# Moving weight sums and token sums of a Strassen-like MLP between stages of a one-core transformer block

## The chip, the cores and the metric

The kernel runs on one core of one Trainium2 chip. The metric is the device time of one execution in microseconds. The profile is of one further execution, whose own time is given beside the time of the others.

## The reference

A conditioned transformer block on x of shape (2, 2048, 512) in float32: two rows of 2048 tokens, width 512 (D), 16 heads of 32, hidden width 2048.

```python
mod = silu(condition) @ Wada + bada
sh_a, sc_a, gt_a, sh_m, sc_m, gt_m = split(mod, 6)
xm = layernorm(x) * (1 + sc_a) + sh_a
x = x + gt_a * attention(xm)          # causal softmax, 16 heads, then @ Wproj + bproj
xm = layernorm(x) * (1 + sc_m) + sh_m
h = gelu(xm @ W1 + b1)                # exact gelu
x = x + gt_m * (h @ W2 + b2)
```

## The kernel before

**Order of the work.** For each row: QKV (in four groups g of 512 tokens), attention, projection. Behind both rows comes the MLP, four times (m = 0 to 3) over 1024 tokens. The order on each engine is written out by hand: `act` and `mm` keep an instruction in program order, and helpers named `among`, `also`, `between` and `then` hang other work behind a numbered step of the main loop. All DMAs on SP are issued in program order too; GpSimd (POOL) issues the others from its own queue, in which its additions stand as well.

**The MLP.** Both layers are block products with seven instead of eight multiplications (the Winograd form of Strassen's scheme), applied twice: seven outer products, named A11, S1, A12, S2, S3, S4, A22 after the weight operand, each of seven inner products (`seven`), each of those 4 weight tiles times 256 tokens. Operands are sums of blocks:

- Weight sums: a piece of a layer has seven blocks, four loaded and three summed in four steps (`room_sum`, L1222, 128x512 in a full room). The outer sums were made earlier and lie in DRAM as `w1d`, `w2d`; complete pieces lie in `w1e`, `w2e`. Three pieces of W1 are completed in row 1's QKV (`FirstLayer`, at steps 1, 7 and 13 of its 48), four in row 1's attention in halves (`FirstHalves`, through `beside`). All seven of W2 are completed in m=0 of the MLP: `Weights.load` fetches four blocks, `Weights.add` puts the four sums on POOL during the outer product before the one that needs them, and then stores the piece in `w2e` for m = 1 to 3. For these, SP loads each piece in two parts.
- Token sums of the first layer: each outer operand needs four inner sums of 128x256 (`inner_x`, 28 for each m). One is made per inner product, for the coming outer product, on POOL, or on VectorE (DVE) while the outer products S3 and S4 (numbers 4 and 5) run.
- Token sums of the second layer (`Hidden`): sums of 128x1024 on DVE (`pop`). Four of them may be made within the first layer, from outer product 5 on, when no inner sum of the coming product is left.

All these sums are recorded at L1586 (`difference`). In the first layer, DVE adds each product's PSUM banks to a tile (`combine`, L1713), two evictions for each inner product. In the outer products S2 and S3, POOL adds every new block to another one (also L1713, `h<-h,h`), and where an eviction is a copy by ScalarE (ACT), POOL makes the addition (L1941, `c<-c,h`). The inner products write to the bank pairs `ps_a`, `ps_b` and `ps_c`; `ps_a` is added to several times, so the seventh inner product waits for the eviction of the fifth, the fifth for that of the third.

**Attention.** For each unit of 512 queries and four heads there are row scores (`s`, for the maxima, DVE reduces them) and transposed scores (`st`, for the exponentials by ACT). Row scores run ahead, in a list `row.todo`; when it is empty there are none left. Each step of 128 keys opens four `st` banks with a small matmul (`st<-fold,sel`) and waits for their last exponentials. `st_bank` gives them four banks, and in the last unit two more, those of `s`. A few row scores run already in QKV: `among` puts them between its matmuls. In the last value product of the last group it left out the place before the last matmul, so that the scores due there came behind it. Row 1's attention keeps its tiles where the rooms of row 1's QKV lay.

Of the kernel before, what the change touches and what calls it, by code (L numbers as in the profile page):

```python
# [17 lines left out]
P = 128  # L18
# [9 lines left out]
def dit_block_kernel(  # L28
# [540 lines left out]
    def attention_phase(row, beside=None):  # L569
        b, vv, kst, qst = row.b, row.vv, row.kst, row.qst  # L570
        with pool(f"att{b}") as ap, pool(
# [7 lines left out]
            def scores_t(u, step, n, behind_rows):  # L579

                def st_bank():

                    n_bank[0] += u == len(units) - 1
                    if n_bank[0] % 6 >= HC:
                        return ps_sp.tile([P, QB], F32, tag="s", name="st")
                    return ps_stp.tile([P, QB], F32, tag="st", name="st")

                c, i = units[u]
                tiles = steps_of[u][step]
                q0 = tiles[0][1]
                w = sum(QB - q for _, q in tiles)
                sts, es = [], []  # L600
                for h in range(HC):
                    g = slice(h * HD, (h + 1) * HD)
                    st = st_bank()
                    mm(
                        st[:, :w], sel[g, :], fold[u % 2][g, q0 : q0 + w],
                        start=True, stop=False,
                    )
                    sts.append(st)
                narrow = w < QB or u == 0
                if n > HC:  # L610
                    row.score(1)
                for h in range(HC):
                    at = 0
                    for j, q in tiles:
                        mm(
                            sts[h][:, at : at + QB - q],
                            kst[c][:, h, j * P : (j + 1) * P],
                            qst[u][:, h, q:],
                            start=False, stop=at + QB - q == w,
                        )  # L620
                        at += QB - q
                    if h % 2 == 0:
                        e = ap.tile([P, 2, QB], F32, tag="e", name="e", bufs=E_BUFS // 2)
                        es.append(e)
                    act(nc.scalar.activation(e[:, h % 2, :w], sts[h][:, :w], AF.Exp))  # L625
                    if tiles[0][0] >= i * TQ and (h % 2 or len(tiles) > 1):

                        if len(tiles) > 1:
                            d = e[:, h % 2, :].rearrange("p (t k) -> p t k", k=P)
                            d = d[:, 0 : TQ : TQ - 1, :]  # L630
                        else:
                            d = e[:, :, :P]
                        act(
                            nc.gpsimd.affine_select(  # L634
                                d, d, pattern=[[0, 2], [1, P]],
                                compare_op=ALU.is_ge, fill=0.0,
                                base=0, channel_multiplier=-1,
                            )
                        )
# [87 lines left out]
            for u, (c, i) in enumerate(units):  # L727
# [5 lines left out]
                for n_step, tiles in enumerate(steps_of[u]):  # L733
# [77 lines left out]
                        pending.append((now + LAG, lambda u=u, o=o, sm=sm: finish(u, o, sm)))  # L811
                    pending.sort(key=lambda p: p[0])
                    if among:
                        among(now, n_step >= i * TQ, u + 1 == len(units))
                    now += 1
            flush(now + LAG)

# [2 lines left out]
    class Qkv:  # L820
# [241 lines left out]
        def run(self, hp, also):  # L1062
# [3 lines left out]
            for g in range(NG):  # L1066
# [104 lines left out]
                )  # L1171
            )

    def beside(pieces):

        def start(pool_):

            room = pool_.tile([P, piece], F32, tag="w7", name="w7")
            todo = []

            def among(now, slack, last):
                if not todo and pieces.left():
                    todo.append((now + 3 if now else 0, "load"))
                elif not todo:
                    return
                after, what = todo[0]
                if now < after:
                    return
                if what == "load":
                    todo.pop(0)  # L1190
                    pieces.load(room, nc.sync)
                    todo[:] = [(now + 3, n) for n in range(4)]
                elif what == "store":
                    todo.pop(0)
                    pieces.store(nc.sync)
                elif slack or last:
                    todo.pop(0)
                    pieces.make((what,))
                    if what == 3:
                        todo.append((now + 1, "store"))  # L1200
# [27 lines left out]
            room[:, 2:6], src.rearrange("p k (i f) d -> p (k i) (f d)", i=2)  # L1228
        )

    class FirstLayer:

        def __init__(self, rooms):
            self.rooms, self.at, self.made, self.stored = rooms, 0, 0, 0

        def load(self):  # L1240

            act(load_blocks(nc.gpsimd, self.rooms[self.at % 2], 1, self.at))
            self.at += 1

        def make(self):

            room = self.rooms[self.made % 2]
            for k in range(4):
                room_sum(room, 1, k)
            self.made += 1  # L1250

        def store(self):

            act(nc.gpsimd.dma_start(w1e[self.stored], self.rooms[self.stored % 2]))
            self.stored += 1

    class FirstHalves:


        def __init__(self, first):  # L1260
            self.at, self.loaded, self.made = 2 * first, [], []

        def left(self):
            return self.at < 14

        def load(self, room, queue):
            n, half = self.at // 2, self.at % 2
            self.at += 1
            w = room.rearrange("p (n d) -> p n d", n=7)
            src = w1d[:, n].rearrange("p k (i f) d -> p (k i) (f d)", i=2)  # L1270
            act(queue.dma_start(w[:, 2:6], src[:, :, half * 2 * P : (half + 1) * 2 * P]))
            self.loaded.append((n, half, w))

        def make(self, steps):

            for step in steps:
                room_sum(self.loaded[0][2], 1, step)
                if step == 3:
                    self.made.append(self.loaded.pop(0))

        def store(self, queue):

            n, half, w = self.made.pop(0)
            act(queue.dma_start(w1e[n][:, :, half * 2 * P : (half + 1) * 2 * P], w))

    def project_phase(row, psum, between):

# [208 lines left out]
    attention_phase(row, beside(quarters))  # L1496
    assert quarters.at == FC and not quarters.loaded and not quarters.made


# [1 line left out]
    with pool("qkv1") as qp, pool("ps_qkv1", bufs=6, space=PSUM) as ps_mm:  # L1501
# [20 lines left out]
        with pool("hl1") as hp:  # L1522
            room = [
                hp.tile([P, 7, C * P], F32, tag=f"w49{n}", name="w49") for n in range(2)
            ]
            late = FirstLayer(room)

            def also(g, n):
                at = g * (C * 2 + MTT) + n
# [9 lines left out]
            assert late.stored == 3  # L1539

    halves = FirstHalves(late.stored)
    attention_phase(row, beside(halves))
    assert not halves.left() and not halves.loaded and not halves.made
    ps_s_cm.__exit__(None, None, None)

# [4 lines left out]
    with ExitStack() as mlp:  # L1550
# [58 lines left out]
        class Weights:  # L1609
# [6 lines left out]
            def load(self, at, part):  # L1616
# [135 lines left out]
        class Hidden:  # L1752
# [110 lines left out]
            def first_layer(self, among):  # L1863
# [37 lines left out]
                def one_outer(at, n, dst, base):  # L1901
# [61 lines left out]

                    def then(k):
                        self.gelu()
                        if todo and todo[0][0] <= at + 1:
                            inner_x(at)
# [277 lines left out]
```

## Time and profile before

| | |
|---|---|
| Runs | 2245.97, 2245.99, 2253.21 us (median 2245.99) |
| Profiled execution, own time | 2247.44 us |
| Its span, mean granted TensorE clock | 2245.7 us, 0.999 |
| TensorE busy | 2224.7 us (99%) |
| DVE, ACT, POOL busy | 1572.5, 977.6, 1301.1 us |
| QKV, attention of row 1 from | 775, 953 us |
| First layer of m=0 from | 1528.8 us |

A row of the timeline has start and duration in us, engine, line, operation, output and inputs, shape and count, and in brackets the idle time before it with what ended it. A row of a group has, behind the bars, busy us and mean ns, and idle time before it.

### The profile page before, as it was taken

To read this page: it belongs to the slowest core of one execution; us is meant where nothing else is said; L and a number is where in the kernel's file an instruction comes from. 1 tells how busy PE (TensorE), PEld (TensorE's weight loads), DVE (VectorE), ACT (ScalarE), POOL (GpSimd) and SP (SyncE) were. 2 spreads that over 40 slices of the span, in tenths; PEclk is the share of its full clock that TensorE was granted. 3 is DMA by queue.
4 is the path that set the end of the run, shared out by engine and by line. 5 is a ranking of instruction groups with operands and counts; after the bars stand their busy time and mean duration, and the time that the engine had idled before them with its cause. 6 is when DMAs were issued, how large, how long until landed. Compare 5 with 4: busy or idle time off the path is not lost.

```text
span 2245.7 us, 34452 instructions
## 1 busy us (share of the span) xinstructions
PE 2224.7 (99%) x12429; PEld 1442.5 (64%) x12429; DVE 1572.5 (70%) x3172; ACT 977.6 (44%) x1909; POOL 1301.1 (58%) x1052
## 2 busy tenths in 40 slices
PE   8999999999999999999999999999999999999999
PEld 3676555555544457655555555447888888888887
DVE  3467777777776526677777777745996876877787
ACT  3334555555555134255555555723422342252230
POOL 4362997989793550079897998373764602602510
PEclk9999999999999999999999999999999999999999
DMA  8769226262245777551623315465466554654643
GB/s 282 248 208 240 61 64 153 55 149 74 66 158 167 246 243 209 165 126 50 149 74 74 99 50 166 148 231 202 145 254 225 190 188 145 216 181 150 217 147 121
DMA packets 144515, 355.66 MB, mean 158 GB/s; under 512 B 14625, under 2 KB 44877, under 8 KB 130649
## 3 DMA queue, kind: packets, MB, share of 16 engines
q1 hardware_dynamic: 137632, 316.72, 47.3%
q0 software_dynamic: 6336, 36.20, 4.4%
q8 instruction: 98, 1.61, 0.3%
q14 instruction: 73, 0.59, 0.1%
q10 hardware_dynamic: 376, 0.55, 0.1%
HBM read 253.80 MB, written 107.48 MB: 161 GB/s over the span
## 4 chain that ended last, share of the span: by engine, by line
PE 93%; DVE 5%; issue 1%; ACT 0%; DMA 0%; ACTq 0%; DVEq 0%
PE st L204 19%; PE ps_a L204 15%; PE o L204 12%; PE s L204 10%; PE ps_b L204 7%; PE ps_o L204 5%; PE ps_v L204 5%; PE sm L204 4%; PE ps_u L204 4%; PE ps_c L204 4%; PE ps_w L204 3%; PE ps_qk L204 3%; PE ps_xt L212 1%; DVE sum L1586 1%; DVE h L1713 1%
## 5 line engine op out<-in xcount | busy, mean ns | idle before, releaser
L625 ACT ACTIVATE e<-st 128x512 f32<-128x512 f32 (+1 forms) x1152 | 570.0, 579 | 384.1 <-PE st L204 348.5
L481 DVE TENSOR_REDUCE mx<-s 128x1 f32<-128x512 f32 x618 | 420.5, 688 | 179.3 <-PE s L204 176.3
L666 POOL TENSOR_TENSOR ee<-ee,e 128x1024 f32<-128x1024 f32 x204 | 480.0, 2385 | 7.4 <-ACT e L625 7.4
L204 PE MATMUL s<-kst,qst 128*128 128x512 f32 (+3 forms) x1028 | 425.2, 417 | 2.7 <-DVE mx L481 1.5
L204 PE MATMUL st<-qst,kst 128*128 128x512 f32 (+3 forms) x1280 | 377.5, 379 | 0.0
L204 PE MATMUL ps_a<-sum,room 128*128 128x256 f32 x1504 | 356.7, 381 | 3.2 <-DVE c L1713 1.5
L204 PEld LDWEIGHTS ps_a<-sum,room 128*128 128x128 f32 x1504 | 280.8, 190 | 52.3 <-issue 6.0
L204 PE MATMUL o<-e,vv 128*32 128x512 f32 (+3 forms) x2560 | 300.8, 537 | 0.0
L204 PEld LDWEIGHTS st<-qst,kst 128*128 128x128 f32 x1280 | 225.6, 188 | 63.4 <-issue 33.7
L476 DVE CUSTOM_DVE_ANT_0 junk<-s,causal 128x128 bf16<-128x128 f32 (+3 forms) x410 | 186.8, 456 | 104.9 <-PE s L204 97.8
L204 PEld LDWEIGHTS s<-kst,qst 128*128 128x128 f32 x1028 | 193.1, 188 | 103.8 <-issue 48.0
L666 POOL TENSOR_TENSOR ee<-e 128x1024 f32<-128x1024 f32 x84 | 198.3, 2383 | 93.5 <-ACT e L625 93.5
L634 POOL TENSOR_SCALAR_AFFINE_SELECT e<-e 128x256 f32<-128x256 f32 x256 | 109.9, 460 | 143.5 <-ACT e L625 142.0
L204 PEld LDWEIGHTS <-sel 32*128 32x128 bf16 x1152 | 29.4, 90 | 190.4 <-issue 186.6
L1941 POOL TENSOR_TENSOR c<-c,h 128x512 f32<-128x512 f32 x40 | 58.6, 1486 | 153.0 <-ACT c L1939 153.0
L204 PE MATMUL ps_b<-sum,room 128*128 128x256 f32 x608 | 143.6, 379 | 0.0
L204 PEld LDWEIGHTS o<-e,vv 128*32 128x32 f32 x2560 | 62.5, 108 | 98.0 <-issue 80.0
L204 PEld LDWEIGHTS ps_b<-sum,room 128*128 128x128 f32 x608 | 115.0, 190 | 15.4
L204 PE MATMUL ps_v<-wqkv,xmT 128*128 128x512 f32 x256 | 123.0, 595 | 0.0
L204 PE MATMUL st<-fold,sel 32*128 32x512 bf16 (+1 forms) x1152 | 119.1, 372 | 0.9
L1586 POOL TENSOR_TENSOR sum<-xm 128x256 f32<-128x256 f32 x16 | 15.3, 955 | 153.1 <-PE ps_a L204 153.1
L481 DVE TENSOR_REDUCE mx<-st 128x1 f32<-128x512 f32 x150 | 102.4, 683 | 0.4
(233 smaller groups left out, 3313.5 us busy)
## 6 DMA issues: line engine op xcount, KB each, us to landing
qst<-q SPq DMA_DIRECT2D x128, 256.0 KB
room<-w1e SPq DMA_DIRECT2D x28, 1024.0 KB
kst<-k SPq DMA_DIRECT2D x24, 1024.0 KB
room<-w1e SPq DMA_DIRECT2D x28, 768.0 KB
room<-w2e SPq DMA_DIRECT2D x21, 1024.0 KB
q<-hl SPq DMA_DIRECT2D x32, 512.0 KB
k<-hl SPq DMA_DIRECT2D x32, 512.0 KB
room<-w2e SPq DMA_DIRECT2D x21, 768.0 KB
```

Source lines behind the costliest of these rows:

```text
L204: return tc.keep_in_program_order(nc.tensor.matmul(*args, **kw))
L212: return tc.keep_in_program_order(nc.tensor.transpose(dst, src, ident[:n, :n]))
L476: nc.vector.tensor_tensor_reduce(junk[:, :w], s[:, :w], causal[:, QB - w :], 1.0, MASKED, ALU.add, ALU.max, m,)
L481: nc.vector.tensor_reduce(m, s[:, :w], axis=AX.X, op=ALU.max)
L625: act(nc.scalar.activation(e[:, h % 2, :w], sts[h][:, :w], AF.Exp))
L634: nc.gpsimd.affine_select(d, d, pattern=[[0, 2], [1, P]], compare_op=ALU.is_ge, fill=0.0, base=0, channel_multiplier=-1,)
L666: act(engine.tensor_tensor(dst, x, y, ALU.add))
L1586: act(engine.tensor_tensor(dst, x, y, ALU.subtract))
L1713: act(engine.tensor_tensor(dst, x, y, ALU.add))
L1941: nc.gpsimd.tensor_tensor(c, c, piece_of(base, i, t, pair), ALU.add)
```

## The change

Four things change. (1) Four pieces of W2 (S2, S3, A22, S4) are completed in row 1's QKV, at steps 27, 31, 36 and 41, by the class that completes the three of W1; in m=0 the MLP loads them complete, in two parts. (2) The inner token sums of the first layer are all made on POOL, two behind each inner product of the outer products A11 and S1; the early `pop`s of the second layer's sums start in outer product 5 once none is left. (3) Transposed scores use six banks as soon as no row score is left. (4) The left-out place for row scores in the last value product is used. The other edits rename classes or pass the same numbers in another way: `beside` with one sum at a time and a gap of 3 makes the sums where it made them.

```diff
                 def st_bank():
-                    n_bank[0] += u == len(units) - 1
+                    n_bank[0] += not row.todo
                     if n_bank[0] % 6 >= HC:
                         return ps_sp.tile([P, QB], F32, tag="s", name="st")
...
                 def among(n, k):
-                    last = 2 * C + MTT - 1
-                    if g == 0 or g == NG - 1 and n == last and k == C - 2:
+                    if g == 0:
                         return
...
+    BEFORE = OUTER[3:]
...
-    class FirstLayer:
+    class Late:
...
         def load(self):
-            act(load_blocks(nc.gpsimd, self.rooms[self.at % 2], 1, self.at))
+            act(load_blocks(nc.gpsimd, self.rooms[self.at % 2], *self.pieces[self.at]))
             self.at += 1
...
-            late_loads = range(1, 19, 6)
+            late_loads = (1, 7, 13, 27, 31, 36, 41)
+            late_pieces = [(1, n) for n in range(3)] + [(2, n) for n in BEFORE]
+            late = Late(room, late_pieces)
...
-                if m or layer == 1:
+                if m or layer == 1 or n in BEFORE:
                     k = slice(0, 3) if part == 0 else slice(3, 7)
                     nc.sync.dma_start(room[:, k], (w1e if layer == 1 else w2e)[n][:, k])
...
-                def inner_x(now):
+                def inner_x():
                     at, k = todo.pop(0)
-                    engine = nc.gpsimd if now not in (4, 5) else nc.vector
...
-                    difference(t[:, k], u, v, engine)
+                    difference(t[:, k], u, v, nc.gpsimd)
...
                     def then(k):
                         self.gelu()
-                        if todo and todo[0][0] <= at + 1:
-                            inner_x(at)
-                        elif at >= 5 and len(self.made) < 4:
+                        for _ in range(2):
+                            if todo and OUTER1[at] in (A11, S1) and (sums or todo[0][1]):
+                                inner_x()
+                        if not todo and at >= 5 and len(self.made) < 4:
                             self.pop()
                         among(at, k)
```

More of the change, by code (lines that the diff above doesn't have):

```diff
@@ L813, in attention_phase @@
                     if among:
-                        among(now, n_step >= i * TQ, u + 1 == len(units))
+                        among(
+                            now,
+                            1 if u + 1 == len(units) else int(n_step >= i * TQ),
+                        )
                     now += 1
@@ L1172, in store, with beside @@
             )
-    def beside(pieces):
+    def beside(pieces, most, gap):
         def start(pool_):
@@ L1179, in start, with among @@
             todo = []
-            def among(now, slack, last):
+            def among(now, slots):
                 if not todo and pieces.left():
-                    todo.append((now + 3 if now else 0, "load"))
+                    todo.append((now + gap if now else 0, "load"))
                 elif not todo:
@@ L1191, in among @@
                     pieces.load(room, nc.sync)
-                    todo[:] = [(now + 3, n) for n in range(4)]
-                elif what == "store":
+                    todo[:] = [(now + gap, n) for n in range(4)]
+                    return
+                if what == "store":
                     todo.pop(0)
                     pieces.store(nc.sync)
[L1196 to L1200, printed above, removed]
+                    return
+                for _ in range(min(slots, most)):
+                    if todo and todo[0][1] in range(4):
+                        what = todo.pop(0)[1]
+                        pieces.make((what,))
+                        if what == 3:
+                            todo.append((now + 1, "store"))
             return among
@@ L1281, in store @@
         def store(self, queue):
-            n, half, w = self.made.pop(0)
-            act(queue.dma_start(w1e[n][:, :, half * 2 * P : (half + 1) * 2 * P], w))
+            layer, n, half, w = self.made.pop(0)
+            dst = (w1e if layer == 1 else w2e)[n]
+            act(queue.dma_start(dst[:, :, half * 2 * P : (half + 1) * 2 * P], w))
     def project_phase(row, psum, between):
@@ L1494, in dit_block_kernel @@
             assert quarters.at == early and not quarters.loaded and not quarters.made
-    attention_phase(row, beside(quarters))
+    attention_phase(row, beside(quarters, 1, 3))
     assert quarters.at == FC and not quarters.loaded and not quarters.made
@@ L1525, in dit_block_kernel @@
             ]
-            late = FirstLayer(room)
             def also(g, n):
@@ L1535, in also @@
                     late.store()
-            late_loads = range(1, 19, 6)
+            late_loads = (1, 7, 13, 27, 31, 36, 41)
+            late_pieces = [(1, n) for n in range(3)] + [(2, n) for n in BEFORE]
+            late = Late(room, late_pieces)
             qkv.run(hp, also)
-            assert late.stored == 3
-    halves = FirstHalves(late.stored)
-    attention_phase(row, beside(halves))
+            assert late.stored == len(late.pieces)
+    halves = Halves([(1, n) for n in range(3, 7)])
+    attention_phase(row, beside(halves, 1, 3))
     assert not halves.left() and not halves.loaded and not halves.made
@@ L1965, in then @@
                         self.gelu()
-                        if todo and todo[0][0] <= at + 1:
-                            inner_x(at)
-                        elif at >= 5 and len(self.made) < 4:
+                        for _ in range(2):
+                            if todo and OUTER1[at] in (A11, S1) and (sums or todo[0][1]):
+                                inner_x()
+                        if not todo and at >= 5 and len(self.made) < 4:
                             self.pop()
```

33 lines of the change are left out of this document (19 added, 14 removed).

## The prediction

> **What bounds the kernel now.** I read the page first, then TensorE's own waits, then its timeline around each place that the diff touches, and last the engines that TensorE waits for there. The page's first lines:
>
> ```profile
> span 2245.7 us, 34452 instructions
> ## 1 busy us (share of the span) xinstructions
> PE 2224.7 (99%) x12429; PEld 1442.5 (64%) x12429; DVE 1572.5 (70%) x3172; ACT 977.6 (44%) x1909; POOL 1301.1 (58%) x1052
> ```
>
> TensorE is busy 2224.7 of 2245.7 us, so all its idle time is 21.0 us, and the change touches neither the number nor the size of its matmuls. Whatever comes or goes is TensorE's stalls, some of them inside rows that count as busy, since a matmul's end is modelled. So I measure stalls from start to start, in the timeline of TensorE. The MLP runs four times over 1024 tokens (m = 0 to 3); these are the starts of m=0's second layer, of m=1, of m=1's second layer and of m=2:
>
> ```profile
> 1615.01 1.89 PE L204 MATMUL ps_a<-h,room 128*128 128x256 f32 x8
> ...
> 1706.61 1.89 PE L204 MATMUL ps_a<-xm,room 128*128 128x256 f32 x8
> ...
> 1796.36 1.89 PE L204 MATMUL ps_a<-h,room 128*128 128x256 f32 x8
> ...
> 1884.47 1.89 PE L204 MATMUL ps_a<-xm,room 128*128 128x256 f32 x8
> ```
>
> The second layer takes 91.60 us in m=0 and 88.11 us in m=1, with the same matmuls: 3.49 us are lost in m=0, the only one in which GpSimd makes the sums of W2 blocks. TensorE's waits in that stretch name VectorE alone:
>
> ```profile
> PE ps_a L204 <- DVE c L1713: 1.5, 2, 0.9
> PE ps_a L204 <- DVE y L1713: 0.7, 1, 0.7
> ```
>
> In the first layer, products of eight matmul records follow each other like this (S3, then S4 from 1590.31, then A22):
>
> ```profile
> 1584.72 1.89 PE L204 MATMUL ps_a<-sum,room 128*128 128x256 f32 x8
> 1586.44 1.89 PE L204 MATMUL ps_c<-sum,room 128*128 128x256 f32 x8
> 1588.47 1.99 PE L204 MATMUL ps_a<-sum,room 128*128 128x256 f32 x8
> 1590.31 1.89 PE L204 MATMUL ps_b<-sum,room 128*128 128x256 f32 x8
> ...
> 1607.73 1.89 PE L204 MATMUL ps_b<-sum,room 128*128 128x256 f32 x8
> 1609.72 1.99 PE L204 MATMUL ps_a<-sum,room 128*128 128x256 f32 x8
> ```
>
> A free step is 1.72 us (1584.72 to 1586.44). In S3 the step before the seventh product is 2.03 and the seventh itself 1.84: 0.43 us lost. In A22 one step is 1.99, and the next loses the same 0.11: 0.38 us. What delays TensorE there is VectorE:
>
> ```profile
> 1586.30 1.52 DVE L1586 TENSOR_TENSOR sum<-xm,sum 128x256 f32<-128x256 f32 x1
> ...
> 1592.23 0.69 DVE L1713 TENSOR_TENSOR c<-h,ps_b 128x512 f32<-128x512 f32 x1 [0.18 <-PE ps_b L204]
> ...
> 1599.34 0.41 DVE L1586 TENSOR_TENSOR sum<-sum,sum 128x256 f32<-128x256 f32 x1
> ...
> 1600.87 1.21 DVE L1586 TENSOR_TENSOR sum<-h 128x1024 f32<-128x1024 f32 x1
> 1602.00 1.27 DVE L1713 TENSOR_TENSOR h<-c,ps_c 128x512 f32<-128x512 f32 x2
> ...
> 1607.86 1.21 DVE L1586 TENSOR_TENSOR sum<-h,sum 128x1024 f32<-128x1024 f32 x1
> ```
>
> An inner sum of 128x256 takes 0.41 us when GpSimd is idle and 1.52 when it is not. GpSimd at that time:
>
> ```profile
> 1571.36 0.73 POOL L1586 TENSOR_TENSOR sum<-sum,sum 128x256 f32<-128x256 f32 x1
> ...
> 1575.20 0.73 POOL L1586 TENSOR_TENSOR sum<-sum,sum 128x256 f32<-128x256 f32 x1
> ...
> 1586.28 10.44 POOL L1713 TENSOR_TENSOR h<-h,h 128x512 f32<-128x512 f32 x8
> 1596.67 2.67 POOL L1941 TENSOR_TENSOR c<-c,h 128x512 f32<-128x512 f32 x2
> ```
>
> GpSimd adds without a pause until 1599.34, 9.0 us into S4. The two engines get in each other's way only where VectorE adds two tiles in SBUF; evictions that read PSUM stay at 0.69. Three groups show it, the first from m=0's second layer with GpSimd summing weights, the second from m=1's without, the third over all four m:
>
> ```profile
> L1586 DVE TENSOR_TENSOR h<-h,h 128x1024 f32<-128x1024 f32 x8 | 15.0, 1883 | 0.0
> ...
> L1586 DVE TENSOR_TENSOR h<-h,h 128x1024 f32<-128x1024 f32 x8 | 9.7, 1217 | 0.0
> ...
> L1586 DVE TENSOR_TENSOR sum<-sum 128x256 f32<-128x256 f32 x8 | 11.4, 1423 | 0.0
> ```
>
> **Four W2 pieces in QKV.** Sixteen block sums, their loads and their stores leave GpSimd's queue in m=0's second layer (pieces S2, S3, A22, S4); SP loads the finished pieces in two parts, as it does in m=1. Three pieces are still summed there, during the outer products A22 of layer 1, A11 and S1, where the profile shows no stall that grows from it. I take the whole difference to m=1: -3.5 us, with a bound of 0 if it were the loads. In QKV the work goes into GpSimd's queue for row 1. There it sat idle 51.2 us before the attention's first mask:
>
> ```profile
> 955.45 0.41 POOL L634 TENSOR_SCALAR_AFFINE_SELECT e<-e 128x256 f32<-128x256 f32 x1 [51.18 <-ACT e L625]
> ...
> L1222 POOL TENSOR_TENSOR w<-w x12: 1262/1267/1274, 788.2 to 836.0; 128x512 f32<-128x512 f32 x12
> ...
> DMA to landing us min/median/max: 5.1/8.3/13.5
> ```
>
> One piece fits ahead of the last token sums, three come behind them, from 904.3 on (955.45 less 51.18): three times four sums of 1.27 are 15.2 us, two loads that are waited for 16.6 at the median, some 3 for issuing: the last store goes out at about 939 and lands at about 947. Queued behind it are the masks, and the third exponential, one of those ahead of these masks, writes a tile over the room that this store reads, at about 955. Cost 0; without that cover see the third rival. VectorE's maxima read PSUM and aren't slowed by these sums.
>
> **Inner token sums early, all on GpSimd.** All 28 stand in GpSimd's queue within the first two outer products: 28 of 0.73 are 20.4 us against 14 steps of 1.72, 24.1 us. Queued behind them are the two additions of A12, needed five steps later: 0. VectorE loses eight sums per m, so S3's 0.43 goes. But what is late next: the four 128x1024 sums for layer 2 may start once no inner sum is left and the product is S4 or later. Before, one of them ran at S4's end and three in A22 with GpSimd idle (1.21 each). Now all four stand in S4, one behind each of the first four products. A22's 0.38 goes, and S4 gets this. Its seventh product starts 10.3 us after S4's start (six steps) and needs the first eviction of the fifth. Without contention VectorE is through the first pair at 2.5 us (1592.23 + 0.69 - 1590.31, less 0.08 overlap), two sums at 1.13 from start to start (1600.87 to 1602.00) 4.8, a pair at 1.20 (two evictions of 0.60) 6.0, a sum 7.1, a pair 8.3, a sum 9.5, the eviction 10.1: no stall, 0.2 to spare. With contention a sum costs more:
>
> ```profile
> 1646.65 2.27 DVE L1586 TENSOR_TENSOR h<-h,sum 128x1024 f32<-128x1024 f32 x1
> ...
> 1649.17 1.95 DVE L1586 TENSOR_TENSOR h<-h,sum 128x1024 f32<-128x1024 f32 x1
> ```
>
> Two neighbours under GpSimd's sums took 2.27 and 1.95, so 1.06 and 0.74 more than 1.21. Does GpSimd still work then? Its 9.0 us into S4 shrink by at most the three or four sums of 0.73 that S2 loses, less because its h sums wait for evictions anyway, and S4 starts 0.43 earlier: it ends some 7 us into S4. When the first of the four sums is ready at 2.5, GpSimd has about 4.5 us, three to four additions, left. They alternate with the first three sums: 2.2 to 3.2 us, 2.0 to 3.0 of it past the spare 0.2. I take 2.4. Bounds: 0 (GpSimd done by then) and 3.7 (the fourth sum meets it too). Per m: 2.4 - 0.43 - 0.38 = +1.6; four m, since the contended sums look alike in all (1423 ns mean of 8): +6.4 us, between -3.2 and +11.6.
>
> A rule speaks against this step too. The Trainium skill, page "SBUF — State Buffer", section "SBUF: two separate sides", says that VectorE with two SBUF inputs and GpSimd take a shared port pair as an exclusive lock, for the whole of an instruction, and that the other blocks. The trace agrees: 2.27 us for a sum of 1.21. Should sums under that rule arrive at random, they would wait half an addition each, which gives a time of its own (second rival).
>
> **No scores put off.** In both rows, at the end of QKV:
>
> ```profile
> 951.38 1.03 PE L204 MATMUL s<-kst,qst 128*128 128x512 f32 x2
> 952.95 0.44 PE L204 MATMUL s<-kst,qst 128*128 128x384 f32 x1 [0.55 <-DVE mx L481]
> 953.32 0.40 PE L204 MATMUL st<-fold,sel 32*128 32x512 bf16 x4
> ...
> 952.03 0.59 ACT L896 COPY vv<-ps_v 128x512 f32<-128x512 f32 x1 [3.44 <-PE ps_v L204]
> ```
>
> Two scores move ahead of the last value matmul, whose two passes then cover the wait of 0.55. But ScalarE's copy of that product, which the third transposed score's bank waits for, ends 0.4 to 0.5 later, near 953.1 instead of 952.62, and the transposed scores began at 953.32. So 0.2 of 0.55 is left, twice: -0.4 us (bounds 0 and -1.1).
>
> **Six banks earlier.** The last row score runs at 664, in the last unit but one; its remaining three steps now use six banks. There the four openers of a step (0.40 when nothing waits) spread:
>
> ```profile
> 664.13 0.40 PE L204 MATMUL s<-kst,qst 128*128 128x512 f32 x1
> ...
> 665.46 0.40 PE L204 MATMUL st<-fold,sel 32*128 32x512 bf16 x4
> ...
> 671.09 0.69 PE L204 MATMUL st<-fold,sel 32*128 32x256 bf16 x4
> ```
>
> The second of these waits goes (0.2 to 0.3); the one before it only moves from the fourth bank to the first, as the row transposes take one of the two added banks. Twice -0.2: -0.4 us (bounds 0 and -1.0).
>
> **Sum.** -3.5 + 6.4 - 0.4 - 0.4 = +2.1 us. The profiled execution took 2247.44 us, so 2249.5 for such a one; the median of the runs shown is 1.45 lower, 2245.99, and so I forecast 2248.1 us. What a measurement of this kernel can tell from no change is 0.5%, 11.2 us; one of its three runs lay 7 us above the others.
>
> **Rivals.** First, GpSimd is done before the four sums start: for it speaks that its queue loses sums, against it that the h sums wait for evictions. Then S4 has no stall: -3.2 - 3.5 - 0.8 = -7.5, 2238.5 us. Second, GpSimd still works, but the sums arrive at random against its additions and wait half of one: 10.44/8 is 1.3, half 0.65, for three sums 1.95, less the spare 0.2 a stall of 1.75. Then 4 x (1.75 - 0.81) - 3.5 - 0.8 = -0.5, 2245.5 us; for it speaks the spread of the 128x256 sums, against it that engines which alternate meet just behind each other's start, as the 2.27 did. Third, the other way: the last W2 store lands late. With 13.5 us for both loads and the store, it lands at 963 instead of 947, and ScalarE's third exponential of row 1, and TensorE behind it, wait up to 8 us: 2256 us. It decides from 955 on; for it speaks that q and k stores and key loads run just then, against it the median of 8.3. Fourth, the change doesn't do what it says: m=0's second layer stays long because of loads and not sums: +3.5, 2251.6 us; against it speaks that all the waits name VectorE.
>
> **How the numbers follow.** Forecast 0.50, first rival 0.17, second 0.15, third 0.08, fourth 0.07, others 0.03. The forecast's own bounds are 2245 to 2252.5; the second and fourth lie inside or near; reaching to the first, and halfway to the third, gives 2238.3 to 2254.0. Faster by over 0.5% needs nearly every stall named here to go and more: 0.02. Slower by over 0.5% needs the third rival on top of the upper bound of S4: 0.04. The rest, 0.94, is no change.
>
> **What would show it.** After the change, m=0's second layer should take 88.1 us; the seventh step of S3 and A22 be 1.72; in S4 the step before the seventh product about 4 us, with the 128x1024 sums on VectorE near 2.2 while GpSimd's c<-c,h of S4 is still running. Sums of 1.21 there, or ScalarE waiting for a store at 955, would make the forecast wrong.

## The result, and the profile after

The changed kernel takes 2255.29 us (median of 12 runs, 2253.14 to 2259.7) against 2247.9 us for the kernel before, timed on the same chip: a ratio of 1.0033, 95% interval 1.0023 to 1.0042. It is 0.3% slower, 7.2 us above the forecast and 1.3 us above the upper end of the range. Of these 7.2 us, 1.9 lie in the kernel before, which the forecast took at 2245.99; the change itself cost 7.4 us where 2.1 were forecast. Its profiled execution took 2254.18 us, 6.7 us more than that of before. The first lines of the page:

```profile
span 2252.4 us, 34503 instructions
...
PE 2222.2 (99%) x12429; PEld 1445.2 (64%) x12429; DVE 1546.7 (69%) x3140; ACT 977.5 (43%) x1909; POOL 1312.5 (58%) x1088
```

The work on TensorE is the same to the instruction. Where the time lies shows in the starts of the MLP's layers, from TensorE's timeline: m=0, its second layer, m=1, its second layer.

```profile
1526.32 1.89 PE L204 MATMUL ps_a<-xm,room 128*128 128x256 f32 x8
...
1616.58 1.67 PE L204 MATMUL ps_a<-h,room 128*128 128x256 f32 x7
...
1706.11 1.24 PE L204 MATMUL ps_a<-xm,room 128*128 128x256 f32 x5
...
1798.18 1.03 PE L204 MATMUL ps_a<-h,room 128*128 128x256 f32 x4
```

- The first layer of m=1 takes 92.07 us (1706.11 to 1798.18); before it took 89.75 (1706.61 to 1796.36). That is 2.32 more per m, 9.3 over four.
- In m=0 it takes 90.26, and by the old starts there (1528.79 to 1615.01) took 86.22: 4.04 more, that is 1.7 on top of the 2.32.
- The second layer of m=0 takes 89.53 instead of 91.60: 2.07 less, where 3.49 were forecast.
- All that lies ahead of the MLP takes 2.47 less (1526.32 against 1528.79).

The sum, 9.3 + 1.7 - 2.07 - 2.47, is 6.5 of the 6.7 us. The 1.7 is a spell of 3.4 us at half clock (last section). The profile of before has such a spell too, from 18.6 us on, at the start of row 0's QKV, and it makes some 1.7 of the 2.47. That the two cancel is luck of these two executions.

TensorE's waits from S4 of m=0 to the middle of its second layer (us in total, times, longest):

```profile
PE ps_a L204 <- DVE h L1722: 2.1, 1, 2.1
PE ps_a L204 <- DVE y L1722: 1.2, 1, 1.2
PE ps_a L204 <- DVE c L1722: 0.5, 1, 0.5
```

The first and the third are S4's stall, the second is new. S4 on TensorE, VectorE and GpSimd, from the timeline of each:

```profile
1587.43 1.89 PE L204 MATMUL ps_b<-sum,room 128*128 128x256 f32 x8
...
1595.10 1.97 PE L204 MATMUL ps_a<-sum,room 128*128 128x256 f32 x8 [0.45 <-DVE c L1722]
1596.90 1.89 PE L204 MATMUL ps_c<-xm,room 128*128 128x256 f32 x8
1600.86 2.96 PE L204 MATMUL ps_a<-sum,room 128*128 128x256 f32 x8 [2.07 <-DVE h L1722]
...
1589.96 2.18 DVE L1595 TENSOR_TENSOR sum<-h 128x1024 f32<-128x1024 f32 x1
1592.18 2.17 DVE L1595 TENSOR_TENSOR sum<-h,sum 128x1024 f32<-128x1024 f32 x1
...
1595.47 2.32 DVE L1595 TENSOR_TENSOR sum<-h,h 128x1024 f32<-128x1024 f32 x1
...
1598.91 1.21 DVE L1595 TENSOR_TENSOR sum<-h,sum 128x1024 f32<-128x1024 f32 x1
...
1587.33 5.94 POOL L1722 TENSOR_TENSOR h<-h,h 128x512 f32<-128x512 f32 x4
1593.23 3.47 POOL L1949 TENSOR_TENSOR c<-c,h 128x512 f32<-128x512 f32 x2
```

S4 starts at 1587.43. Three of the four sums take 2.17 to 2.32 us, as long as GpSimd adds (until 1596.70, 9.3 us into S4); the fourth, behind it, takes 1.21. The step from the sixth to the seventh product is 3.96 us (1596.90 to 1600.86). This is the picture that the prediction drew, with two differences: GpSimd ends 9.3 us into S4 and not some 7, and there is a second, smaller stall ahead of the fifth product, of 0.61 us (1595.10).

### The profile page after: what moved, and what is told of

The parts are those of the page before. It is cut to its first block, busy times and chain, and to the rows that moved or that the text cites. A ratio compares the mean times of both kernels' runs of the same rounds, so it can differ in the third digit from the quotient of the medians.

```text
span 2252.4 us, 34503 instructions
## 1 busy us (share of the span) xinstructions
PE 2222.2 (99%) x12429; PEld 1445.2 (64%) x12429; DVE 1546.7 (69%) x3140; ACT 977.5 (43%) x1909; POOL 1312.5 (58%) x1088
## 4 chain that ended last, share of the span: by engine, by line
PE 55%; issue 2%; DVE 2%; ACT 0%; POOL 0%; DVEq 0%; POOLq 0%; ACTq 0%
PE ps_a L204 17%; PE st L204 10%; PE ps_b L204 8%; PE o L204 6%; PE s L204 4%; PE ps_c L204 4%; PE ps_o L204 2%; PE sm L204 2%; DVE sum L1595 1%; PE ps_o L212 1%; PE ps_xt L212 1%; DVE h L1722 0%; ACT e L625 0%; DVE c L1722 0%; DVE fold L554 0%
## 5 line engine op out<-in xcount | busy, mean ns | idle before, releaser
L1595 POOL TENSOR_TENSOR sum<-xm 128x256 f32<-128x256 f32 x24 | 23.3, 970 | 202.5 <-PE ps_a L204 202.5
L1949 POOL TENSOR_TENSOR c<-c,h 128x512 f32<-128x512 f32 x40 | 54.0, 1371 | 134.0 <-ACT c L1947 134.0
```

The costliest lines, as they stand in the source:

```text
L1595: act(engine.tensor_tensor(dst, x, y, ALU.subtract))
L1949: nc.gpsimd.tensor_tensor(c, c, piece_of(base, i, t, pair), ALU.add)
```

## The experiments

Two theories were open. The lock: a sum on VectorE and an addition on GpSimd keep each other out, and only sums that meet additions cost something. The work: four sums beside a product's evictions are too many for VectorE wherever they stand.

**The four sums held to A22 (pops_a22).**

```diff
-                        if not todo and at >= 5 and len(self.made) < 4:
+                        if not todo and at >= 6 and len(self.made) < 4:
```

> The changed kernel, but the four 128x1024 sums for the second layer may start only in outer product A22 (before: at the end of S4; changed: from S4's first step). Theory (lock): the stall of S4 is made by these sums meeting GpSimd's remaining additions; in A22 GpSimd is idle and a sum takes 1.21 us. S4 then loses 0.13 per m and not 3.11, A22 some 0.4 and not 0.13: 4 x (-2.7) = -10.8, and the half-clock spell behind m=0's stall (1.7) goes too: a profiled time of about 2241.7 instead of 2254.18. Rival (work): four sums beside a product's evictions are too much for VectorE wherever they stand: A22 gets the stall of 3 us, and the time stays at 2254. Rival (scatter): S4 has little to do with it, the gap between the two kernels is clock and transfers: 2250 or more.

Measured: 2246.99 us, a ratio of 1.0 (0.9991 to 1.0009): 8.3 less than the changed kernel (7.4 by the ratios), but 5 more than the lock theory gave. S4 has no stall left. The stall went to A22, smaller, and for a reason that I had not looked for. VectorE and GpSimd in A22 of m=0:

```profile
1602.07 1.22 DVE L1595 TENSOR_TENSOR sum<-h 128x1024 f32<-128x1024 f32 x1
1603.32 2.18 DVE L1595 TENSOR_TENSOR sum<-h,sum 128x1024 f32<-128x1024 f32 x1
1606.62 2.33 DVE L1595 TENSOR_TENSOR sum<-h,h 128x1024 f32<-128x1024 f32 x1
1610.08 2.33 DVE L1595 TENSOR_TENSOR sum<-h,sum 128x1024 f32<-128x1024 f32 x1
...
1602.99 3.65 POOL L1949 TENSOR_TENSOR c<-c,h 128x512 f32<-128x512 f32 x2 [8.36 <-ACT c L1947]
...
1606.60 6.93 POOL L1228 TENSOR_TENSOR room<-room 128x512 f32<-128x512 f32 x4
```

"GpSimd is idle in A22" was wrong: behind A22's second product it makes two additions of c, and in m=0 the block sums of W2's first piece. One sum met an addition in m=1 to 3, three did in m=0; A22 loses 1.07 us in m=1 to 3 and 3.30 in m=0.

**GpSimd without its additions behind S3 (no_h_adds).**

```diff
-                        if n not in (S2, S3):
+                        if n != S2:
                             return
```

> The changed kernel, but GpSimd's four additions of 128x512 behind outer product S3's two pairs of tiles (h<-h,h; all that it does behind S3's evictions) are left out in the first layer, so the output lacks them; the four sums of 128x1024 stay in S4. Theory (lock): with GpSimd idle but for two additions of c, the sums take 1.21 us, S4 loses at most 0.3 per m instead of 3.11: 4 x (-2.8) - 1.7 for the spell, about 2241 us. Rival (work): VectorE's own load makes the stall: S4 stays at 3 us per m and the time at 2254.

The edit leaves out eight additions for each m, not four. Measured: 2243.78 us, 0.9988 (0.9979 to 0.9997). S4 loses 1.06 us and not 3.11. S4 of m=1:

```profile
1769.58 1.22 DVE L1595 TENSOR_TENSOR sum<-h 128x1024 f32<-128x1024 f32 x1
1770.83 2.18 DVE L1595 TENSOR_TENSOR sum<-h,sum 128x1024 f32<-128x1024 f32 x1
...
1774.13 1.21 DVE L1595 TENSOR_TENSOR sum<-h,h 128x1024 f32<-128x1024 f32 x1
...
1776.46 1.21 DVE L1595 TENSOR_TENSOR sum<-h,sum 128x1024 f32<-128x1024 f32 x1
...
1770.56 3.58 POOL L1949 TENSOR_TENSOR c<-c,h 128x512 f32<-128x512 f32 x2 [8.49 <-ACT c L1947]
```

The same four sums stand at the same places, and one is long: the one that meets the two additions of c. It is 0.97 over the others. In the changed kernel the three long ones are together 3.04 over 1.21 (0.97 + 0.96 + 1.11), and S4 loses 3.11. So each sum that meets an addition costs TensorE about what it is longer by, and the work of four sums by itself next to nothing. The bound of 0.3 was missed by that one sum; the work theory, which had 3 us here, falls.

**One part alone (w2_only, inner_only, w2_scores).** w2_only is the kernel before with only `BEFORE`, `Late` and the seven `late_loads`; inner_only is it with only the hunks of `inner_x` and `then`; w2_scores is the changed kernel with these two hunks put back.

> The kernel before with the W2 pieces S2, S3, A22 and S4 summed in QKV alone; inner sums, banks and late scores as before. Recorded forecast of this term: -3.5 us (m=0's second layer at 88.1 us instead of 91.6): 2243.9. Theory now (late load): with S1's blocks landing 8 us after the issue, GpSimd makes S1's and A12's sums back to back and a new wait of 1.4 us in S1 takes part of it back: second layer 89.6, -2.0: 2245.4. Rival: that wait came out of the early inner sums, and here the whole -3.5 shows. Rival: the sums in QKV cost as much as they save there: 2247.4.

> The kernel before with the early inner token sums, all on GpSimd, and the pops from S4's first step alone. Recorded forecast of this term: +6.4 us. Theory now: S4 loses 3.05 us more per m and not 2.4, S3 and A22 give 0.40 and 0.30 back: 4 x 2.3 = +9.3, so 2256.7, and 1.7 more if a half-clock spell follows m=0's stall. Second layer of m=0 stays at 91.6. Rival (scatter): the sums cost the forecast 6.4, 2253.8, and the rest of the difference between the kernels is clock.

> The changed kernel with the inner token sums as before (so W2 pieces in QKV, six banks, no scores put off). Recorded forecast for these three terms: -3.5 - 0.4 - 0.4 = -4.3, 2243.1 for a profile like the 2247.44 of before. Against the kernel with the W2 pieces alone (2242.09 median) the recorded terms say -0.8: 2241.3; rival: the banks and scores give nothing or cost up to 0.5: 2242.1 to 2242.6. In m=0 the second layer takes 88.1 us, S4's stall is 0.07.

Measured: w2_only 2242.09 us, 0.9986 (0.9977 to 0.9995); inner_only 2259.13, 1.0056 (1.0044 to 1.0069); w2_scores 2242.3, 0.9979 (0.9970 to 0.9988). Starts of m=0's second layer and of m=1 in w2_only, then in inner_only:

```profile
1613.90 1.89 PE L204 MATMUL ps_a<-h,room 128*128 128x256 f32 x8
...
1702.01 1.24 PE L204 MATMUL ps_a<-xm,room 128*128 128x256 f32 x5
```

```profile
1618.15 1.03 PE L204 MATMUL ps_a<-h,room 128*128 128x256 f32 x4
...
1710.89 1.46 PE L204 MATMUL ps_a<-xm,room 128*128 128x256 f32 x6
```

Alone, the W2 pieces bring the second layer to 88.11 us, the forecast -3.5 in full. Alone, the early inner sums make it 92.74, 1.1 longer than before: the new stall in S1 (1.47 us here) belongs to them and not to the W2 pieces. With both, it takes 89.53 in the changed kernel, so on top of the inner sums the W2 pieces still gave 3.21. So "late load" was the wrong owner in my expectation of w2_only, and its rival was right. In S4 inner_only loses 3.12 us in every m, as the changed kernel does. The medians add up: -4.4 and +12.6 against the common 2246.5, with the forecast -0.8 for banks and late scores, give +7.4, and +7.4 was measured.

The banks and late scores: from QKV's first matmul to the MLP's first, w2_only takes 1508.77 us (18.93 to 1527.70) and w2_scores 1507.62 (18.14 to 1525.76). That is 1.15 less in one execution each; the medians (2242.09 and 2242.3, timed at different times) don't resolve it. QKV gives 0.81 of it in row 0 (183.21 to 182.40) and 0.19 in row 1; attention and projection get 0.20 longer in row 0 and 0.37 shorter in row 1. The wait of 0.55 for the maxima did give way to one for the copy of the last value product, as forecast; row 1 in w2_scores:

```profile
951.06 0.40 PE L204 MATMUL st<-fold,sel 32*128 32x512 bf16 x4 [0.55 <-ACT vv L899]
```

**Why S1 stalls: the order of a store and a load (store_sp, store_behind).** In the kernel before, SP's load of S1's blocks went out at 1615.20, 0.37 ahead of GpSimd's store of A11's piece, and S1's block sums began at 1621.63:

```profile
1615.20 0.32 SPq L1227 DMA_DIRECT2D room<-w2d  x1
...
1615.57 0.60 POOL L1638 DMA_DIRECT2D w2e<-room  x1 [0.30 <-POOL room L1222]
1621.63 7.92 POOL L1222 TENSOR_TENSOR room<-room 128x512 f32<-128x512 f32 x4 [5.46 <-DMA room<-w2d]
```

In the changed kernel the store is first, by 1.09:

```profile
1615.68 0.59 POOL L1647 DMA_DIRECT2D w2e<-room  x1 [0.30 <-POOL room L1228]
1625.23 7.89 POOL L1228 TENSOR_TENSOR room<-room 128x512 f32<-128x512 f32 x4 [8.96 <-DMA room<-w2d]
...
1634.01 7.94 POOL L1228 TENSOR_TENSOR room<-room 128x512 f32<-128x512 f32 x4
...
1616.77 0.32 SPq L1233 DMA_DIRECT2D room<-w2d  x1
```

The load now takes 8.5 us until its sums start, not 6.4, and A12's sums (1634.01) follow S1's with no pause but the store's issue; in the kernel before 1.83 us lay between. VectorE's own sums meet additions for 16 us on end, and the stall is TensorE's wait for VectorE's `y` (1.2 us, above). Two kernels put the store on SP's queue to turn the order back.

```diff
-                    nc.gpsimd.dma_start(w2e[n], rooms[at % 2])
+                    if n == A11:
+                        self.held.append((w2e[n], rooms[at % 2]))
+                    else:
+                        nc.gpsimd.dma_start(w2e[n], rooms[at % 2])
...
+                if self.held:
+                    nc.sync.dma_start(*self.held.pop())
```

> The changed kernel, but the store of W2's first summed piece (A11) goes out on SP's queue, behind the load of S1's blocks, instead of on GpSimd's queue as soon as its sums are done. In the kernel before, the load was issued 0.37 us ahead of that store and landed after 6.3 us; in the changed one 1.09 us behind it, and landed after 8.3. Theory (queue order): the 1.41 us stall in S1 of m=0's second layer comes from this: S1's sums start 2 us later and run straight into A12's. With the load first it lands after some 6.3 us, the stall goes, m=0's second layer takes 88.1 us, and the time is 1.4 less than the changed kernel's: 2252.8 for a profile like its 2254.18. Rival (contention): the stall comes from VectorE's sums being slowed for longer, whatever the load does: it stays, second layer 89.5, no change. S4's stall of 3.1 per m stays by both.

Measured: 2256.28 us, 1.0041 (1.0028 to 1.0055). The edit didn't do what it was for: the load isn't wrapped in `act`, which keeps an instruction in program order, and the store still came first:

```profile
1617.18 0.32 SPq L1672 DMA_DIRECT2D w2e<-room  x1
1618.54 0.67 SPq L1233 DMA_DIRECT2D room<-w2d  x1
```

S1 loses 1.36 us. This doesn't tell the theories apart, but it is the control for the next run: the store is on SP's queue here too, and the stall stays. In store_behind both transfers are held in the order in which they are written:

```diff
-                    load_blocks(nc.sync, room, layer, n)
+                    act(load_blocks(nc.sync, room, layer, n))
...
-                    nc.sync.dma_start(*self.held.pop())
+                    act(nc.sync.dma_start(*self.held.pop()))
```

> As the run before on this question, whose edit left the load behind the store (load at 1618.54, store at 1617.18, landed 7.7 us after its issue), but now SP's queue is held in order: S1's load first, then the store of A11's sums. Theory (queue order): the load, first again, lands after some 6.3 us, S1's sums start at least 1.5 us sooner, S1's stall of 1.4 in m=0's second layer goes (88.1 us); time 1.4 below the changed kernel's, 2253.9 for its median of 2255.29. Rival (contention): VectorE's sums meet GpSimd's in any case, the stall stays at 1.3 to 1.4 and the second layer at 89.5; no change. S4 stays at 3.1 per m by both.

Measured: 2254.5 us, 1.0030 (1.0019 to 1.0041).

```profile
1623.45 7.92 POOL L1228 TENSOR_TENSOR room<-room 128x512 f32<-128x512 f32 x4 [7.79 <-DMA room<-w2d]
...
1633.90 8.57 POOL L1228 TENSOR_TENSOR room<-room 128x512 f32<-128x512 f32 x4 [1.65 <-DMA room<-w2d]
...
1617.04 0.32 SPq L1233 DMA_DIRECT2D room<-w2d  x1
1617.45 0.38 SPq L1672 DMA_DIRECT2D w2e<-room  x1
```

The load is first by 0.41, S1's sums start 6.4 us behind its issue, a pause of 1.65 is back ahead of A12's, and S1's stall is gone: no outer product of m=0's second layer loses anything. GpSimd makes the same sums and VectorE too, so contention alone, the rival, doesn't make the stall. VectorE's five sums in a row in front of S1's evictions (`sum<-sum,sum` three times, `h<-h,h` twice) take 6.38 and 4.49 us in the changed kernel, 5.30 and 3.42 here. The timed runs (1.0030 against 1.0033) can't resolve 1.4 us; the profiles show it.

The other profiles agree. Where S1's load was issued ahead of A11's store (before, w2_only, w2_scores, store_behind), S1's sums began 6.4 us behind the load's issue, and S1 lost nothing. Where the store was ahead (the changed kernel, inner_only, pops_a22, no_h_adds, store_sp), it was 7.9 to 8.5 us, and S1 lost 1.4 to 1.5.

**A version that keeps the gains (spread, five, spread_behind, spread_again).** spread puts the four sums where GpSimd has nothing to add, and lets QKV sum A11 instead of S2, so that no block sums stand beside A22:

```diff
-                        if not todo and at >= 5 and len(self.made) < 4:
+                        if (at, k) in ((5, 4), (6, 0), (6, 2), (6, 4)):
...
-    BEFORE = OUTER[3:]
+    BEFORE = (A11, S3, A22, S4)
```

> The changed kernel with two edits: the four 128x1024 sums of the first layer stand apart, behind S4's sixth-from-first step (its fifth product) and behind the first, third and fifth product of A22, where GpSimd's additions are over; and QKV sums W2's pieces A11, S3, A22, S4 instead of S2, S3, A22, S4, so that GpSimd has no W2 sums beside m=0's A22, and no store goes out ahead of S1's load. Theory (lock and places): with no sum meeting an addition, S3, S4 and A22 lose 0.13 each per m against 0.53, 0.07 and 0.43 before: -0.6 per m, -2.6; the W2 pieces -3.5 as alone, banks and late scores -0.8: 6.9 less than before, 2239.6 median. Rival (work): four sums are too many for VectorE beside the evictions, each place loses up to 1.07 as A22 did with four in a row: +0.4 per m and not -0.6: 2243.8. Rival (W2): S2's sums now meet VectorE's sums in A12 and S2 of m=0 and stall as S3 and A22 did (2 to 3 us): 2242.

Measured: 2240.43 us, 0.9970 (0.9959 to 0.9981). S3, S4 and A22 lose 0.13 or 0.14 in every m, as forecast; A12 of m=0's second layer loses 1.35, half of what the third expectation gave. A fifth piece in QKV was to end that:

```diff
-    BEFORE = (A11, S3, A22, S4)
+    BEFORE = (A11, A12, S3, A22, S4)
...
-            late_loads = (1, 7, 13, 27, 31, 36, 41)
+            late_loads = (1, 7, 13, 19, 27, 31, 36, 41)
```

> The kernel with the four sums spread over S4 and A22 and W2's A11, S3, A22, S4 summed in QKV, with a fifth piece, A12, summed there too (load at also's place 19). In that kernel m=0's outer product A12 of the second layer lost 1.35 us, with GpSimd summing W2's A12 and S2 beside VectorE's sums. Theory: with A12's sums gone GpSimd sums S1 and S2 with a pause between, no stall is left: m=0's second layer 88.1 us, 1.35 below 2240.43, 2239.1. Rival: the stall stays, since S2's sums alone meet VectorE's in A12: 2240.4. Rival: the fifth piece holds up GpSimd's queue in QKV (its loads, sums and store take some 16 us there): 2242 or more.

Measured: 2243.53 us, 0.9979 (0.9970 to 0.9988). A12's stall went, but row 1's QKV got 2.9 us longer than in the profile of spread (180.77 against 177.88), with one wait of TensorE for which the profile names no releaser. The time is that of the third expectation, but no wait names GpSimd's queue, as it would have it. The fifth piece's load went out at 838.01, among QKV's stores of q and k, and took 12.2 us to land; SP issued the loads of `qst` and `kst` from 850.09 on, in spread from 844.88. That the score, which reads these two tiles, waited for them is not shown, and why the fifth piece makes the wait stays open.

```profile
PE s L204 <- issue: 2.6, 1, 2.6
```

The other way is the order of transfers again: spread, with the stores of S1 and A12 held behind the next load, as in store_behind.

> The kernel with the four sums spread over S4 and A22 and W2's A11, S3, A22, S4 summed in QKV, and now the stores of W2's S1 and A12 in SP's queue behind the next piece's load. Theory (queue order): in that kernel S1's store went out 0.98 us ahead of A12's load, A12's sums came late and S2's stood next to them, which cost 1.35 us in A12 of m=0; with the load first the stall goes: second layer 88.1 in m=0, 2239.1 median. Rival: A12's stall is S2's sums alone, whenever A12's end, and stays: 2240.4. Rival: the store of a piece behind a load now holds up the x loads on SP, and m=0's normalization for m=1 is late: 2241 or more.

> The same kernel as the run named spread (sums spread, W2's A11, S3, A22, S4 in QKV), timed again beside the one above: 2240.4 expected, 0.9970 of the kernel before; the one above 1.3 below it by the theory of queue order, equal to it by the rival.

Measured together: spread_behind 2239.59 us, 0.9958 (0.9945 to 0.9970); spread_again 2241.13, 0.9963 (0.9949 to 0.9976). The intervals overlap, but the profiles don't leave it open: A12 loses 1.35 us in spread_again and nothing in spread_behind. Three of the four sums of m=0 in spread_behind (the fourth took 1.22 too), and the starts of its second layer and of m=1 (88.11 us):

```profile
1597.37 1.22 DVE L1595 TENSOR_TENSOR sum<-h 128x1024 f32<-128x1024 f32 x1
...
1602.55 1.22 DVE L1595 TENSOR_TENSOR sum<-h,sum 128x1024 f32<-128x1024 f32 x1
...
1609.74 1.22 DVE L1595 TENSOR_TENSOR sum<-h,sum 128x1024 f32<-128x1024 f32 x1
...
1612.25 1.46 PE L204 MATMUL ps_a<-h,room 128*128 128x256 f32 x6
...
1700.36 1.46 PE L204 MATMUL ps_a<-xm,room 128*128 128x256 f32 x6
```

No sum is long any more. This version beats both kernels: 0.4% below the one before, and by the ratios (0.9958 and 1.0033) 0.7% below the changed one.

## Why the prediction was wrong, point by point

- **Inner sums, +6.4 forecast: the step that failed, in two places.** The mechanism in S4 was right: sums moved from A22 into S4, where they alternate with GpSimd's additions.
  - The size of S4's stall was too small. I took 2.4 us, by "2.2 to 3.2, 2.0 to 3.0 past the spare 0.2". Three sums were longer by 3.04 together, each near the upper price of the two rows that I had (1.06), none near the lower (0.74), and no spare was left: S4 loses 3.11 against 0.07. S3 and A22 (outside m=0) gave back 0.72 and not 0.81, since each still loses 0.13. Per m the net is +2.32 instead of +1.6, 2.9 us in all. This is the larger of the two.
  - What the same sums do to m=0's second layer was put at nothing. "Queued behind them are the two additions of A12, needed five steps later: 0" looked for what the moved sums delay, not for what they let go earlier. With VectorE's sums out of A22, GpSimd finished A11's block sums 1.20 us before A22's end (1615.38 against 1616.58) and not 0.26 behind it (1615.27 against 1615.01), and its store overtook SP's load. That a store can overtake was in none of the steps; it cost 1.4 us.
- **W2 pieces, -3.5 forecast.** Right: 88.11 us in w2_only. The second layer's -2.07 in the changed kernel is this term less the 1.4 us of the inner sums.
- **Sum of these.** 2.9 and 1.4 are 4.3 us; 2.1 + 4.3 is 6.4, and the profiled executions differ by 6.7.
- **QKV's extra work, 0 forecast.** Right. Row 1's QKV takes 178.06 us in w2_only and 178.07 before, its attention got no longer, and ScalarE waits for no store at 955; the third rival didn't happen.
- **No scores put off and six banks, -0.8 forecast.** Between the two profiles the time ahead of the MLP fell by 2.47, of which the spell at half clock in the profile of before took some 1.7 (row 0's QKV takes 184.95 us there and 183.21 in w2_only, which has the same order of scores and no spell); about -0.8 is left, and -1.15 by w2_scores against w2_only. The total came near by luck, its parts did not: late scores gave 1.0 and not 0.4, six banks 0.2 and not 0.4, by one execution each and too small for the timed runs.
- **Rivals.** The second rival's rule, the shared port pair as an exclusive lock (the Trainium skill, page "SBUF — State Buffer", section "SBUF: two separate sides"), is borne out by these runs: a 128x1024 sum that meets an addition takes 2.17 to 2.33 us, and 1.21 or 1.22 where none runs. What fell is the rival's random arrival with half an addition of wait: the three sums waited about 1.0 each. The first rival, GpSimd done before the four sums, is near to what no_h_adds and spread make by hand: one sum in four meets additions and S4 loses 1.06, or one sum alone stands in S4, meets none, and S4 loses 0.13.
- **The bound on top.** 2254.0 reached halfway to the third rival. S4's own upper bound (3.7) did hold the 3.04 more that it lost. Over four m that bound alone gives 2248.1 + 5.2 = 2253.3, more than the 2252.5 that the prediction names as the forecast's own bound: the terms' bounds were not added up. S1's new wait came on top, and the kernel before was 1.9 us slower in the later runs; against the 2245.99 that it was reckoned from, 2254.0 allowed 8.0 us, and the change cost 7.4.

## What to carry to other kernels

Before work is moved within an outer product, list what the other engine (GpSimd for VectorE) adds in the new place and in the old, product by product: a 128x1024 sum that costs 1.2 us costs 2.2 beside additions, and in S4 TensorE paid nearly all of each such meeting. When work leaves a stretch, ask also what finishes earlier there, and which transfer then goes out ahead of one that somebody waits for; the order of two issues 1 us apart decided 1.4 us. And a part that gains alone (0.1 to 0.2% here) should be timed alone before it is bundled with one that loses.

## What the runs showed of the hardware that was not expected

**A short stall can halve the clock.** The windows of the changed kernel right behind S4's stall in m=0 (length, busy time of each engine, the granted clock, DMA share and GB/s):

```profile
1601.70:1605.10 3.40, 3.40 (x10) 2.66 (x9) 2.09 (x4) 0.00 (x0) 0.00 (x0) 0.50 0.22 31
```

And around a longer wait of w2_only (S3 of m=1, 2.35 us):

```profile
1754.40:1769.50 15.10, 12.75 (x58) 10.43 (x57) 14.54 (x17) 1.17 (x2) 12.15 (x11) 1.00 0.38 122
```

In the first, TensorE ran at half its clock for 3.4 us, which cost the extra 1.7 us of m=0's first layer. The wait ahead of it was 2.07 us. The same stall in m=1 to 3 had no such spell; over the profiles of the changed kernel, inner_only, store_sp and store_behind, four of the 16 stalls did. Length alone doesn't decide it: w2_only's two waits of 2.35, one of 2.94 in pops_a22 and one of 2.56 in five had no spell either.

What separates them is where the wait falls. In each of these traces the granted clock changes only at whole multiples of 3.413 us from its first change (in the changed kernel 1587.20 us, 465 times, then 3.41 and 645.12, 189 times). In the four cases with a spell the whole wait, 2.07 or 2.08 us, lies within one such step, and the spell is the next step. In the other 16 waits the step that holds most of the wait has 2.00 us of it or less. So between 2.00 and 2.07 idle us of a 3.413 us step decided here; four cases are few for a limit so sharp.

The Trainium skill, page "TensorE: Matmul & The Clock Gate", section "Part 1: The HAM clock gate (the "warmup" mystery)", puts the return to the half rate behind at least one idle window of about 3.4 us; here it came behind a wait of 2.07 us within a step, and the measurement decides. None of the profiles without S4's long stall (before, w2_only, w2_scores, no_h_adds, pops_a22, spread, spread_again, five, spread_behind) has a spell after the first 25 us and before the last 6.

**A short sum can wait for five additions in a row.** VectorE, GpSimd and TensorE in S3 of m=1 in w2_only:

```profile
1756.93 5.83 DVE L1596 TENSOR_TENSOR sum<-xm 128x256 f32<-128x256 f32 x1
...
1752.62 7.41 POOL L1723 TENSOR_TENSOR h<-h,h 128x512 f32<-128x512 f32 x6
1760.00 2.48 POOL L1951 TENSOR_TENSOR c<-c,h 128x512 f32<-128x512 f32 x2
...
1763.96 1.97 PE L204 MATMUL ps_a<-sum,room 128*128 128x256 f32 x8 [2.35 <-DVE c L1723]
```

A sum of 0.41 us was over only when GpSimd had finished the addition in progress and four more, and S3 lost 2.94 us instead of 0.5; it happened in m=1 and m=2 of this execution and in m=0 and m=3 didn't. This execution took 2247.39 us, 5.3 more than the median, and the two losses make 4.9 of it. The runs of w2_only spread from 2241.57 to 2247.39, those of spread, which has no 128x256 sum on VectorE any more, from 2239.06 to 2240.91. That such losses make the spread of the kernel before as well is argued from this, not shown.
